# The next image's layer 0 is paced by a line with bends instead of a fixed lead

## The chip, the cores and the metric

The kernel runs on one core of a Trainium2 chip. The metric is the device time of one launch in microseconds. A core has five engines with a queue of their own each: PE (TensorE, matrix products), DVE (VectorE), ACT (ScalarE), POOL (GpSimd) and SP (SyncE, which here only issues DMAs). PEld in the profile is PE's loading of weights, which overlaps its products.

## The reference

The input is four images of 32 by 32 pixels with 384 channels in float32. Four layers follow one another, each of the form `x = x + layer(group_norm(x))`:

```python
x = x + L0(_gn(x))  # deformable attention, 6 heads of 64: q = x@w_q; a grouped 3x3 convolution of q,
                    # LayerNorm, GELU and tanh give an offset per pixel and group; x is sampled
                    # bilinearly there; k, v from the samples;
                    # softmax(q k^T * scale + bias sampled from a table) v; @ w_out
x = x + L1(_gn(x))  # attention, 12 heads of 32, softmax(q k^T) times a weight from sim sim^T, where
                    # sim = sigmoid(cosine of pixels with a strided depthwise convolution), renormalised; @ Wproj
x = x + L2(_gn(x))  # quotient of two box sums (5 pixels along a row, 20 channels)
x = x + L3(_gn(x))  # outlook attention: 9x9 weights per pixel from a softmax, values gathered and
                    # scattered over 3x3 neighbourhoods
```

The layers of one image depend on each other; the images do not.

## The kernel before

All work is written out by Python generators and is unrolled. There are two **lanes**. The front lane (`Front`) computes layer 0. The trunk lane (`Trunk`) computes layers 1 to 3. Image 0 goes through the front lane alone. Then the trunk of image b is issued together with the front of image b+1, for b = 0, 1, 2; the trunk of image 3 runs alone at the end. The front hands its result over in device memory (`x1`): `outputs0` stores it and `Trunk.start` loads it.

A lane is a generator that issues some instructions and then yields a number, its own account of how much it has issued. `Net.layer3` drives both. After each yield of the trunk it adds the number to `done` (as a share of `TRUNK_STEPS` = 1109) and then lets the front issue steps until `ahead` (in shares of `FRONT_STEPS` = 714) has reached a target that depends on `done`. One trunk image is 1.0 of `done`, one front image 1.0 of `ahead`. The order in which instructions are issued here is their priority: a scheduler at compile time keeps to it where it can and lets a later instruction pass one that isn't ready by its own clock. On the chip each engine then works through its list in the fixed order.

The trunk's yields sum up like this (cumulative share of `done` at the end of each stage):

| trunk stage | code | numbers | `done` at its end |
|---|---|---|---|
| norm of x1 | `image` | 15 | 0.0135 |
| inputs of layer 1: Wg product (L400) with depthwise taps on DVE, q, k, v (L1216, L414), norms through device memory | `inputs1` | 158 | 0.156 |
| six pairs of heads, 8 rows of keys each (L1511, L1519, L1541, L1548, L1483), beside the sums for the next pair (L1378, L1386, L1387) | `pair` | 708 | 0.794 |
| output product of layer 1 (L1614) | `out1` | 18 | 0.811 |
| layer 2 (L1656, L1681) | `layer2` | 93 | 0.8945 |
| layer 3: norm, weights and values (L414), sums of weights (L1790), a round trip through device memory (`mt<-skew`), then eight output blocks (L1849) | `layer3` | 15, 30, 20, 20, 8 x 4 | 1.0 |

`Trunk.start(b + 1)` is issued before the eight output blocks.

The front's steps of one image are, in order: `normed` (25: load, transposes L585, group norm), transposes and stores of the sampling source `pairs` (10, L608), q (3 x 5, L400), the grouped convolution (3 x 15, L663), LayerNorm and GELU (25), `positions` (20: about 50 DVE instructions), the first two gathers (8), eight blocks of gather, weighing on DVE and transposes (8 x 7, L735, L748, L762), k and v (30). This is step 234. Then twelve passes of `head0` (one head, half of the queries each): eight blocks (3 each) with a gather by POOL (L827), L840, L844, L845, the product L848 and L849 on DVE; the maximum (3); subtraction L880, exp L881 and products L883 (4 x 2); a store (3). After each second head `over_sums` (2) sends the denominators through device memory and scales (L1128). This is step 696. `outputs0` (3 x 6) applies w_out (L400 `big<-qpad,w`), adds x and stores x1.

Image 1 differs: its `normed` has already been done beside the heads of image 0.

Of the kernel before, what the change touches and what calls it, by code (L numbers as in the profile page):

```python
# [58 lines left out]

TRUNK_STEPS, FRONT_STEPS, LEAD = 1109.0, 714.0, 0.1


def bc(ap, axis, n):
# [7 lines left out]
class Net:  # L73
# [212 lines left out]
    def layer3(self, b, out):  # L286

        for w in self.trunk.image(b, out):
            self.done += w / TRUNK_STEPS
            while self.ahead < self.done + LEAD:  # L290
                self.ahead += next(self.fronts, FRONT_STEPS) / FRONT_STEPS
        assert self.ahead >= min(b + 1, NB - 1)

# [1650 lines left out]
```

## Time and profile before

| | |
|---|---|
| median of 3 runs | 4535.31 us (4531.07 to 4537.83) |
| the profiled execution's own time | 4532.7 us |
| its span, first to last instruction | 4530.9 us |
| busy: PE, DVE, ACT, POOL | 90%, 69%, 51%, 21% |
| mean granted TensorE clock | 0.945 |

The span falls into image 0's front alone (to about 550 us), three stretches of a trunk with the next front (the first Wg product of a trunk stands at 592.5, 1695.3, 2799.9 and 3841.3 us), and the last trunk alone. Every float32 product of 128 x 512 is recorded as two matmul instructions, so a "x24" is twelve products. A matmul's end is modelled and its duration includes the pipeline, so that neighbours in a row overlap; "busy" is the union.

### The profile page before, as it was taken

The numbers are of one execution on the slowest core, as the hardware profiler recorded it, in microseconds if no ns is written. First come the engines' busy times: TensorE is split into PE (matmuls) and PEld (weight loads), VectorE is DVE, ScalarE is ACT, GpSimd is POOL, SyncE is SP. The second block draws the span as 40 slices with busy tenths as digits, with TensorE's granted clock in tenths as the row PEclk, the third lists the DMA queues.
The fourth block names the chain that finished last, engine by engine and source line by source line (L and its number), as shares of the span: only waits on it lengthen the run. The fifth ranks groups of instructions, "written<-read, shape, count | busy, mean of one in ns | idle before, by whom it ended". The sixth has DMA issues, their size and how long they took to land.

```text
span 4530.9 us, 46955 instructions
## 1 busy us (share of the span) xinstructions
PE 4084.6 (90%) x15672; PEld 1735.9 (38%) x15672; DVE 3133.6 (69%) x5925; ACT 2302.5 (51%) x3633; POOL 967.5 (21%) x978
## 2 busy tenths in 40 slices
PE   5599889999999898999999989899999998999998
PEld 2233334333334353433333344343333334344444
DVE  4599555878787727677878753777787874566654
ACT  2176333666665414556666332356566641466632
POOL 1654223212112104211212010422121311000000
PEclk8799899999999998999999989899999998999998
DMA  6445234322212244321322124532122213411011
GB/s 141 145 138 137 80 115 126 86 55 67 67 50 66 73 135 143 110 55 55 85 55 79 39 85 124 164 97 59 43 76 55 78 38 115 121 29 38 22 41 42
DMA packets 235923, 377.28 MB, mean 83 GB/s; under 512 B 117763, under 2 KB 167264, under 8 KB 235680
## 3 DMA queue, kind: packets, MB, share of 16 engines
q1 hardware_dynamic: 183640, 207.55, 16.3%
q0 software_dynamic: 39936, 145.53, 10.9%
q10 hardware_dynamic: 12104, 21.19, 1.4%
q8 instruction: 124, 2.03, 0.2%
q14 instruction: 119, 0.97, 0.1%
HBM read 294.19 MB, written 80.27 MB: 83 GB/s over the span
## 4 chain that ended last, share of the span: by engine, by line
PE 57%; DVE 14%; ACT 6%; issue 6%; DMA 4%; POOL 1%; SPq 0%; another core or an unknown queue 0%; ACTq 0%; DVEq 0%; POOLq 0%
PE bank L1541 13%; PE big L1511 5%; PE big L400 4%; PE bank L414 4%; PE bank L883 4%; PE big L1378 4%; PE bank L848 4%; PE bank L1483 3%; PE bank L1536 3%; PE bank L1216 2%; DVE nmax L1386 2%; ACT big L1387 2%; DVE e L1548 2%; PE big L663 2%; DVE lg L849 1%
## 5 line engine op out<-in xcount | busy, mean ns | idle before, releaser
L1541 PE MATMUL bank<-whole,sg 128*128 128x512 f32 (+3 forms) x2304 | 845.3, 500 | 2.0 <-POOL sg L1494 2.0
L1548 DVE SCALAR_TENSOR_TENSOR e<-bank,gam,e 128x512 f32<-128x512 f32 x768 | 560.5, 747 | 312.5 <-PE bank L1541 176.3
L1387 ACT ACTIVATE big<-big,nmax 128x1024 f32<-128x1024 f32 x384 | 417.5, 1087 | 276.1 <-DVE nmax L1386 264.1
L1519 ACT ACTIVATE e<-big 128x1024 f32<-128x1024 f32 x384 | 380.6, 1019 | 325.5 <-PE big L1511 319.5
L1541 PEld LDWEIGHTS bank<-whole,sg 128*128 128x128 f32 x2304 | 398.2, 195 | 348.1 <-issue 259.7
L1386 DVE TENSOR_REDUCE nmax<-big 128x1 f32<-128x1024 f32 x384 | 452.9, 1218 | 66.8 <-PE big L1378 52.3
L827 POOL DMA_INDIRECT win<-strips,widx x288 | 324.1, 1125 | 706.5 <-DVE z L840 352.2
L1511 PE MATMUL big<-qa,ka 64*128 64x512 f32 x1536 | 432.6, 643 | 22.7 <-ACT big L1387 21.8
L1494 POOL TENSOR_SCALAR sg<-whole,gam 128x512 f32<-128x512 f32 x192 | 143.9, 750 | 1317.3 <-PE bank L1541 1057.7
L1378 PE MATMUL big<-k,q 32*128 32x512 f32 x1536 | 283.4, 654 | 40.9 <-ACT big L1387 21.3
L848 PE MATMUL bank<-qpad,kz 128*128 128x512 f32 x576 | 283.4, 620 | 9.8 <-ACT gn L1553 8.3
L735 POOL DMA_INDIRECT gat<-pairs,sidx x192 | 207.4, 1080 | 385.0 <-DVE ix_gt L516 207.2
L883 PE MATMUL bank<-lg,va 128*64 128x512 f32 x576 | 266.7, 607 | 24.8 <-ACT lg L881 24.8
L883 PE MATMUL bank<-lg,ones 128*64 128x512 f32 x576 | 266.1, 607 | 0.0
L845 DVE SCALAR_TENSOR_TENSOR lg<-z,bias_f,lg 128x512 f32<-128x512 f32 x288 | 218.5, 772 | 58.8 <-ACT lg L844 56.2
L1511 PEld LDWEIGHTS big<-qa,ka 64*128 64x128 f32 x1536 | 138.0, 190 | 278.0 <-issue 123.2
L1483 PE MATMUL bank<-e,vs 128*32 128x512 f32 x1536 | 230.8, 619 | 8.7 <-DVE vs L1477 8.4
L839 ACT ACTIVATE z<-win,bias_f 128x528 f32<-128x528 f32 x288 | 203.6, 735 | 41.6 <-DVE lg L845 21.9
L840 DVE SCALAR_TENSOR_TENSOR z<-win,bias_f,z 128x528 f32<-128x528 f32 x288 | 214.2, 761 | 9.0 <-issue 6.5
L880 DVE TENSOR_TENSOR lg<-lg,tb 128x512 f32<-128x512 f32 x288 | 186.9, 700 | 45.9 <-ACT tb L873 45.9
L849 DVE TENSOR_TENSOR lg<-bank,lg 128x512 f32<-128x512 f32 x288 | 192.1, 684 | 37.6 <-PE bank L848 37.2
L844 ACT ACTIVATE lg<-z,bias_f 128x512 f32<-128x512 f32 x288 | 201.1, 716 | 12.3 <-PE bank L883 5.0
(311 smaller groups left out, 6494.3 us busy)
## 6 DMA issues: line engine op xcount, KB each, us to landing
pairs<-xn SPq DMA_DIRECT2D x64, 192.0 KB
q<-qd SPq DMA_DIRECT2D x48, 256.0 KB
xg<-xgd SPq DMA_DIRECT2D x48, 256.0 KB
w<-in_gmat SPq DMA_DIRECT2D x16, 576.0 KB
w<-in_w_off SPq DMA_DIRECT2D x12, 576.0 KB
w<-in_Wqkv SPq DMA_DIRECT2D x12, 576.0 KB
a<-in_x SPq DMA_DIRECT2D x16, 384.0 KB
x<-a ACTq DMA_DIRECT2D x4, 1536.0 KB
```

Source lines behind the costliest of these rows:

```text
L827: nc.gpsimd.indirect_dma_start(out=win, out_offset=None, in_=self.strips[:, :], in_offset=bass.IndirectOffsetOnAxis(ap=self.widx[:, q, c : ...
L848: nc.tensor.matmul(ps, kz[:, j * P : (j + 1) * P], both, start=True, stop=True)
L849: v.tensor_tensor(lf, ps, lf, ALU.add)
L883: nc.tensor.matmul(po[out, :], w, lf, start=j == 0, stop=j == NJ - 1)
L1378: nc.tensor.matmul(ps[r][:, h * 512 : (h + 1) * 512], self.q4[rows, i * P : (i + 1) * P], self.k4[rows, 0:512], start=True, stop=True,)
L1386: v.tensor_reduce(nmax[:, r, i : i + 1], ps[r], AX.X, ALU.max, negate=True)
L1387: nc.scalar.activation(ps[r], ps[r], AF.Exp, bias=nmax[:, r, i : i + 1], accum_out=den[:, r, i : i + 1],)
L1483: nc.tensor.matmul(av[r0 : r0 + HD1, :], vs[:, r, :], es[h][:, r, :], start=j == 0, stop=j == NJ - 1,)
L1511: nc.tensor.matmul(ps[:, r, :], ka[rows, j * P : (j + 1) * P], qa[rows, cols], start=True, stop=True,)
L1519: nc.scalar.activation(e, ps, AF.Exp)
L1541: last = nc.tensor.matmul(ps[:, (mid - i0) * P :], sg[:, r, m, :], sim[:, h, r, m, (mid - i0) * P :], start=m == 0, stop=m == 1,)
L1548: v.scalar_tensor_tensor(e[:, r, :], ps, self.gam[:, 1:2], e[:, r, :], ALU.add, ALU.mult, accum_out=tot[:, r, h : h + 1],)
```

## The change

Only the target of the front lane changes. Before, it is `done + 0.1` everywhere. After, it is piecewise linear within each image of the trunk. No instruction is added or taken away; their order of issue changes.

```diff
-TRUNK_STEPS, FRONT_STEPS, LEAD = 1109.0, 714.0, 0.1
+TRUNK_STEPS, FRONT_STEPS = 1109.0, 714.0
+PACE = ((0.0, 0.156, 0.795, 0.96, 1.0), (0.03, 0.14, 0.80, 1.0, 1.03))
...
         for w in self.trunk.image(b, out):
             self.done += w / TRUNK_STEPS
-            while self.ahead < self.done + LEAD:
+            share = float(np.interp(self.done - b, *PACE))
+            while self.ahead < b + share:
                 self.ahead += next(self.fronts, FRONT_STEPS) / FRONT_STEPS
```

In front steps (714 to an image; above 714 they belong to the image after the next) the two targets are:

| end of the trunk's stage | `done` | target before | target after |
|---|---|---|---|
| start of the image | 0 | 71 | 21 |
| norm | 0.0135 | 81 | 28 |
| inputs of layer 1 | 0.156 | 183 | 100 |
| pairs | 0.794 | 639 | 571 |
| layer 2 | 0.8945 | 710 | 657 |
| layer 3, weights and values | 0.935 | 739 | 692 |
| layer 3, sums of weights | 0.953 | 752 | 708 |
| layer 3, round trip issued | 0.971 | 765 | 720 |
| end of the image | 1.0 | 785 | 735 |

## The prediction

> **What bounds the kernel now.** I read the page first, then busy time by stage (windows cut at the first Wg product, the first L1541 and the first L1614 of a trunk), then the chain of waits at the ends of the stages, then the waits in the first one.
>
> ```profile
> PE 4084.6 (90%) x15672; PEld 1735.9 (38%) x15672; DVE 3133.6 (69%) x5925; ACT 2302.5 (51%) x3633; POOL 967.5 (21%) x978
> ...
> PE 57%; DVE 14%; ACT 6%; issue 6%; DMA 4%; POOL 1%; SPq 0%; another core or an unknown queue 0%; ACTq 0%; DVEq 0%; POOLq 0%
> ```
>
> PE is first, but holds the chain for only 57% of it. The windows (columns: stretch, length, then busy us of PE, PEld, DVE, ACT, POOL; granted clock; DMA) give the second trunk with a front (rows 1 to 3: inputs of layer 1, pairs, tail), the tail of the third trunk, where no further front follows (row 4), and the last trunk alone (rows 5 to 7):
>
> ```profile
> 1695.30:1828.70 133.40, 114.50 (x328) 48.32 (x324) 98.42 (x172) 57.95 (x96) 60.06 (x61) 0.86 0.50 151
> 1828.70:2558.20 729.50, 683.03 (x2724) 275.04 (x2722) 573.64 (x1126) 449.53 (x716) 152.22 (x153) 0.97 0.24 67
> 2558.20:2799.90 241.70, 212.49 (x831) 106.45 (x827) 116.42 (x195) 66.72 (x94) 22.90 (x15) 0.91 0.32 98
> 3663.50:3841.30 177.80, 157.89 (x516) 79.25 (x513) 105.97 (x176) 53.27 (x70) 14.50 (x9) 0.93 0.25 79
> 3841.30:3939.50 98.20, 95.91 (x281) 39.93 (x281) 47.14 (x73) 41.79 (x66) 9.51 (x16) 0.97 0.44 139
> 3939.50:4382.40 442.90, 438.10 (x2072) 187.83 (x2070) 279.14 (x661) 265.00 (x416) 31.97 (x46) 1.00 0.11 28
> 4382.40:4527.80 145.40, 117.52 (x380) 63.88 (x376) 70.50 (x115) 37.76 (x43) 11.32 (x7) 0.87 0.17 52
> ```
>
> So the front costs 133.4 - 98.2 = 35 us beside the inputs, 729.5 - 442.9 = 287 beside the pairs, 241.7 - 145.4 = 96 in the tail. Alone, inputs and pairs are PE's (98 and 99% busy); the tail leaves PE 28 us and DVE 75 us idle. In the tail with a front, PE has work of the front on the chain:
>
> ```profile
> 1647.29 10.30 PE big L400 x24
> 1657.59 7.89 PE big L663 x72
> 1665.47 9.23 PE bank L1849 x28
> 1674.70 7.89 PE big L663 x72
> 1682.59 3.42 PE bank L1849 x10
> 1686.01 1.46 PE bank L355 x14
> 1687.47 7.89 PE big L663 x72
> ...
> 2158.51 7.02 PE bank L883 x32
> ```
>
> q (L400) and the three convolutions (L663) stand between the trunk's output blocks (L1849) and its Wg, on a full PE: q's 36 records at 10.30/24 = 0.43 are 15.5 us, the convolutions 3 x 7.89 = 23.7, together 39.
>
> Beside the inputs of layer 1 it is different. PE waits there, among others:
>
> ```profile
> POOL gat L735 <- DVE ix_gt L516: 50.4, 1, 50.4
> ...
> PE bank L762 <- DVE xn L751: 10.0, 1, 10.0
> ```
>
> All 48 gathers lie in that window. POOL waits for the positions, DVE for the gathers, and PE's first transpose of the samples for DVE, with the trunk's products behind it in PE's list.
>
> A pass of the heads, by the groups of the page (columns: shapes, count, busy us, mean ns, idle before) and the last line of the chain above:
>
> ```profile
> L845 DVE SCALAR_TENSOR_TENSOR lg<-z,bias_f,lg 128x512 f32<-128x512 f32 x288 | 218.5, 772 | 58.8 <-ACT lg L844 56.2
> L840 DVE SCALAR_TENSOR_TENSOR z<-win,bias_f,z 128x528 f32<-128x528 f32 x288 | 214.2, 761 | 9.0 <-issue 6.5
> L880 DVE TENSOR_TENSOR lg<-lg,tb 128x512 f32<-128x512 f32 x288 | 186.9, 700 | 45.9 <-ACT tb L873 45.9
> L849 DVE TENSOR_TENSOR lg<-bank,lg 128x512 f32<-128x512 f32 x288 | 192.1, 684 | 37.6 <-PE bank L848 37.2
> ```
>
> DVE: 8 x (0.772 + 0.761 + 0.700 + 0.684) = 23.3, with seven maxima of 0.69 and one reduction of 0.7, 29 us. PE: L883 7.0, L848 16 records at 0.43 = 6.9, the maximum's transposes and product 1.3: 15 us. In the trace the pairs run 125 us each with about two passes beside them (77 alone), that is 227 us for ten passes, **22.7 us a pass**. In the tail of row 4, one pass by its DVE work (16 of L880, 10 of L849) and w_out's 36 records (15.5 us) cost 177.8 - 145.4 = 32.4: **17 us a pass**.
>
> A rule bears on this: the Trainium skill, "Perfetto Trace Analysis", section Identifying the Most-Contended Engine, says that the busy share of matmuls is a poor measure of how near PE is to its limit, since matmuls are pipelined. The rows agree: L848 has a mean of 620 ns and a spacing of 0.43 us. Taken at its busy time, PE in the pairs would have 46 us to give and no more.
>
> **The change, part by part.** Instructions and their durations stay. In front steps the targets are 71 before and 21 after at an image's start, 183 and 100 after the inputs, 639 and 571 after the pairs, 785 and 735 at the end. So three packets move, in each of the three stretches:
>
> 1. Steps 21 to 71 (end of `normed`, `pairs`, q, most convolutions) go from the tail to the inputs of the next trunk. Tails 1 and 2 lose 39.6 us of PE on the chain: -79. The first Wg of all (592.5) had q and convolutions ahead of it, 16.6 and 23.3 us of the chain; part of that filled the wait for the norm, so -30.
> 2. Steps 100 to 183 (LayerNorm, `positions`, five of eight gathers; in the trace all gathers) go from the inputs to the pairs. The inputs lose their 35 and gain the 39 of q and convolutions, since PE is full there alone: +4 each, +12. They cost the pairs between 7 (their PE work, two sets of 24 transposes) and 45 (56 us of the front's DVE work in that window at the pairs' 22.7/29). Nearest is the 35 that they cost beside the inputs, with PE's wait of 10 in it; the pairs are longer and the chain has other work beside it, so I take 25.
> 3. 68 steps, that is 68/38.5 = 1.76 passes, go from the pairs to the tail. The pairs give back 1.76 x 22.7 = 40. With the 25 that is -15 each, -45; ends -33 and +5.
>
> The passes' price p in the tail is not in the trace. Half of the 1.76 falls into layer 2 and half into layer 3. From below it is PE's 15, or 10 if layer 3's round trip and norm, where PE waits anyhow, take part of it; from above DVE's 29, or 35 with the waits inside a pass (top, diag, ones, copy: about 4) and a third of `over_sums` (about 6). A gain below zero has no reason, since nothing falls away. I take the 17 of row 4, the same stage: three tails x 1.76 x 17 = +90.
>
> Sum: -30 + 12 - 45 - 79 + 90 = **-52**; as a formula -142 + 5.28 p, zero at p = 27. The profiled execution was 4532.7, so 4481; the median of the runs is 2.6 above it: **4483**.
>
> What is queued where: SP takes the chain of `over_sums` and the x1 stores and reloads amid layer 3's `skew` and `mt` transfers; they used to come during layer 2. Trunk norm, then Wg, wait for x1, now stored just before `start` loads it. In the first stretch that chain, from the store at 539.0 to the end of the group matmuls at 552.6, is 14 us. I cost it at nothing: the output blocks of layer 3 (14 to 15 us of L1849) and its transposes lie beside it. Without that cover it is 14 to 18 in each of three tails. POOL's `sg` for the trunk's rows stands behind 48 gathers of 1.08 us in the pairs now; POOL is 21% busy there, so nothing, unless a gather waits for positions as above.
>
> One rule speaks against the change: the Trainium skill, "TensorE: Matmul & The Clock Gate" (table at its head), has the queues of VectorE, ScalarE and GpSimd as strictly first in, first out. A head's instruction that waits then holds layer 2's behind it. The wait of PE on L762 shows the effect of a fixed order; that DVE has it in layer 2 no row shows. By the rule p would be near 35 and the sum +43.
>
> **The rivals.**
> *DVE sets the tail (slower).* Layer 2 runs serially through DVE, ACT and PE, and a pass is first of all DVE work. In row 4 DVE is busy 106 of 178; with 1.76 passes more, 51 us, and nothing else, it would be 157 of some 208. If each pass goes in series, p = 35: -142 + 185 = +43, **4578**. It decides above p = 27. For it: in row 4's chain, DVE's L849 and L854 alternate with layer 2's. Against it: row 4 measured 17.
> *The lanes pack better.* Pairs hold input work spread over them in place of lumps, and give 30 each; layer 3 hides part of the passes, p = 15: -30 + 12 - 90 - 79 + 79 = -108, **4427**. For it: pair 0 takes 136 us now, the longest, with front steps in lumps of 20 to 30. Against it: the pairs' PE is 94% busy.
> *Nothing happens.* The scheduler lets ready work pass, so the actual order follows readiness rather than the targets: **4535**. Against it: q and convolutions stand in the trace where the target puts them. For it: all gathers ran ahead of theirs.
>
> **How the numbers follow.** The forecast (4440 to 4526) has 0.40, better packing 0.18, no difference 0.09, DVE in the tail 0.33, in which I count the x1 handoff and POOL's order too. A measurement here tells about 0.2%, or 9 us: faster 0.58, same 0.09, slower 0.33. The lower end takes p = 15, the pairs' -33 (-117) and a little more, the upper end p = 35: 4405 to 4578.
>
> **What would show it.** Right: the first Wg at about 562; stretch of the inputs 134 to 140 with PE over 95% busy and no gathers in it; pairs near 715; tails of the first two trunks near 232, of the third near 208. Wrong: DVE above 85% in the tail with longer L1656 to L1681 stretches; `whole<-x` or a PE wait on L355 on the chain ahead of Wg; POOL `sg` late for L1541 in pairs 0 and 1.

## The result and the profile after

The changed kernel takes 4717.27 us (median of 4 runs, 4714.41 to 4719.14) against 4536.06 for the kernel before on the same chip: a ratio of 1.0397, with a 95% interval of 1.0383 to 1.0411. It is slower by 181 us; 52 us faster had been forecast. The profiled span grew by 186 us, from 4530.9 to 4717.2. The changed file is two lines longer ahead of every line named here, so L400 is now L402 and L1849 is L1851.

Page of the kernel after: busy time by engine, then the chain that ended last, by engine.

```profile
PE 4130.1 (88%) x15672; PEld 1738.8 (37%) x15672; DVE 3126.9 (66%) x5925; ACT 2312.9 (49%) x3633; POOL 972.0 (21%) x978
...
PE 51%; DVE 15%; issue 8%; ACT 8%; DMA 4%; POOL 2%; another core or an unknown queue 1%; SPq 0%; DVEq 0%; ACTq 0%; POOLq 0%
```

The instruction counts are the same to the last one, and the busy times nearly so. What changed is the chain: PE has gone from 57% to 51% of it. No engine got more instructions; PE waits more.

Windows of the kernel after, cut at the same places as before (second trunk with a front; tail of the third; last trunk alone):

```profile
1721.50:1872.10 150.60, 141.33 (x563) 58.09 (x563) 65.52 (x107) 61.39 (x101) 9.07 (x16) 0.97 0.46 131
1872.10:2614.90 742.80, 660.85 (x2595) 263.67 (x2594) 540.24 (x1078) 410.01 (x654) 176.66 (x175) 0.95 0.22 62
2614.90:2886.50 271.60, 219.00 (x716) 107.15 (x715) 179.70 (x308) 105.86 (x153) 51.33 (x38) 0.86 0.31 98
3778.80:4026.90 248.10, 206.43 (x659) 96.39 (x658) 172.55 (x290) 101.08 (x142) 46.48 (x35) 0.88 0.30 92
4026.90:4125.60 98.70, 96.41 (x282) 40.00 (x282) 47.10 (x73) 42.10 (x66) 9.49 (x16) 0.97 0.44 142
4125.60:4568.60 443.00, 438.47 (x2070) 187.75 (x2069) 279.15 (x660) 264.39 (x415) 31.82 (x46) 1.00 0.11 27
4568.60:4714.10 145.50, 117.79 (x380) 63.68 (x376) 70.65 (x117) 37.74 (x43) 11.38 (x7) 0.87 0.17 52
```

The last trunk alone is unchanged. In the second stretch the inputs went from 133.4 to 150.6 us, the pairs from 729.5 to 742.8, the tail from 241.7 to 271.6. In the pairs PE has 22 us less to do and the stage is 13 us longer all the same. In this tail the granted clock is lower too, 0.86 against 0.91. That is not the main reason for its growth: of two runs below (e1 and e2), both with 0.90 in this tail, one takes 66 us longer than the other. Over the whole run (first Wg at 552.5):

| | first Wg | inputs 1, 2, 3 | pairs 1, 2, 3 | tails 1, 2, 3 | last trunk |
|---|---|---|---|---|---|
| before | 592.5 | 134.9, 133.4, 135.1 | 730.8, 729.5, 728.6 | 237.1, 241.7, 177.8 | 686.5 |
| after | 552.5 | 150.4, 150.7, 150.1 | 744.6, 742.8, 742.3 | 274.0, 271.6, 248.1 | 687.2 |
| sum of differences | -40 | +48 | +41 | +137 | +1 |

The chain of waits of the kernel after, ahead of the second trunk's Wg (start, length, what):

```profile
1641.89 4.44 PE bank L1792 x36
...
1649.06 4.63 DMA skew<-urow
1653.71 4.41 DMA lg<-rden
...
1658.89 10.17 PE big L402 x16
...
1670.80 4.21 DMA res<-x
...
1676.51 4.03 DMA x<-res
...
1681.11 5.92 DMA a<-in_x
1687.04 0.04 issue
1687.08 4.11 PE bank L587 x18
...
1697.14 3.12 PE bank L357 x14
1700.25 17.18 PE bank L1851 x44
```

Before, q and the convolutions stood between the output blocks there. They are gone: the 44 output blocks run as one piece of 17 us. In their place there is now what the front must do to hand x1 over: denominators (`lg<-rden`), w_out (L402 here), the store and reload of x1, then the next image's load and norm, one after another, 47 us from the first of these to the output blocks.

Chain of the kernel after in the next tail, during layer 2:

```profile
2670.06 1.20 DVE lg L851 x2
2671.26 0.60 DVE rmax L856
2671.86 1.20 DVE t L1651
2673.06 0.60 DVE rmax L856
2673.66 1.20 DVE t L1670
2674.86 0.60 DVE lg L851
2675.47 1.13 DVE d L1671
```

The front's L851 and L856 and layer 2's L1651, L1670, L1671 take turns on DVE, and all of them are on the chain. The window from the output product to Wa, the first product of layer 3, shows how full DVE is there; before first, then after:

```profile
2558.20:2693.00 134.80, 112.79 (x326) 50.80 (x323) 89.93 (x130) 47.88 (x62) 20.27 (x12) 0.92 0.23 78
```

```profile
2614.90:2770.00 155.10, 123.56 (x356) 51.24 (x356) 130.34 (x204) 83.92 (x113) 45.40 (x34) 0.89 0.24 76
```

DVE is busy for 130.3 of 155.1 us, 84%; it was 67%.

The gathers (POOL's timeline of the kernel after: start, us, instruction, idle before it) are now in the first pair, where POOL also makes the trunk's `sg` rows:

```profile
1890.98 1.12 POOL L737 DMA_INDIRECT gat<-pairs,sidx  x1 [9.09 <-DVE ix_gt L518]
...
1912.42 0.95 POOL L737 DMA_INDIRECT gat<-pairs,sidx  x1 [0.30 <-issue]
1913.40 0.70 POOL L1496 TENSOR_SCALAR sg<-whole,gam 128x512 f32<-128x512 f32 x1
1926.31 0.69 POOL L1496 TENSOR_SCALAR sg<-whole,gam 128x512 f32<-128x512 f32 x1 [12.20 <-PE bank L1543]
```

Eighteen gathers run without a break, 1.25 us from start to start, and one `sg` stands behind them. The chain of the same kernel at that place:

```profile
1903.14 1.21 ACT big L1389 x2
1904.35 12.18 another core or an unknown queue
1916.55 1.03 ACT e L1521
1917.62 3.00 PE big L1380 x5
```

There is one core here, so "another core" is a wait whose releaser the records do not give. It ends 2.5 us after that `sg`, and no product of PE is recorded between the two. So that the `sg` is what was waited for is read from the order of the instructions; run e4 below tests it. PE waited 10.9 us ahead of 1917.62. A second run of eighteen gathers from 1972.33 holds two more `sg` until 1997.55, and PE waits 4.6 us.

### The profile page after: what moved, and what is told of

Same layout as the page of the kernel before. It is cut to its first block, busy times and chain, and to the rows that moved or that the text cites. A ratio compares the mean times of both kernels' runs of the same rounds, so it can differ in the third digit from the quotient of the medians.

```text
span 4717.2 us, 46931 instructions
## 1 busy us (share of the span) xinstructions
PE 4130.1 (88%) x15672; PEld 1738.8 (37%) x15672; DVE 3126.9 (66%) x5925; ACT 2312.9 (49%) x3633; POOL 972.0 (21%) x978
## 4 chain that ended last, share of the span: by engine, by line
PE 51%; DVE 15%; issue 8%; ACT 8%; DMA 4%; POOL 2%; another core or an unknown queue 1%; SPq 0%; DVEq 0%; ACTq 0%; POOLq 0%
PE bank L1543 11%; PE big L1513 6%; PE big L402 4%; PE bank L885 4%; PE big L1380 3%; PE bank L850 3%; PE bank L416 3%; DVE nmax L1388 3%; PE bank L1538 3%; PE bank L1485 2%; ACT big L1389 2%; PE bank L1218 2%; DVE e L1550 2%; DVE z L842 2%; PE big L665 2%
## 5 line engine op out<-in xcount | busy, mean ns | idle before, releaser
L1543 PE MATMUL bank<-whole,sg 128*128 128x512 f32 (+3 forms) x2304 | 850.3, 502 | 14.0 <-issue 12.3
L1388 DVE TENSOR_REDUCE nmax<-big 128x1 f32<-128x1024 f32 x384 | 453.4, 1219 | 186.8 <-PE big L1380 177.3
L1543 PEld LDWEIGHTS bank<-whole,sg 128*128 128x128 f32 x2304 | 399.0, 196 | 371.4 <-issue 281.2
L1496 POOL TENSOR_SCALAR sg<-whole,gam 128x512 f32<-128x512 f32 x192 | 133.5, 696 | 1801.2 <-PE bank L1543 1079.5
L829 POOL DMA_INDIRECT win<-strips,widx x288 | 344.0, 1194 | 772.9 <-DVE z L842 423.7
L1513 PE MATMUL big<-qa,ka 64*128 64x512 f32 x1536 | 446.5, 665 | 48.0 <-ACT big L1389 46.3
L1380 PE MATMUL big<-k,q 32*128 32x512 f32 x1536 | 297.7, 660 | 69.4 <-ACT e L1521 39.0
L885 PE MATMUL bank<-lg,va 128*64 128x512 f32 x576 | 289.8, 649 | 38.9 <-ACT lg L883 38.8
L850 PE MATMUL bank<-qpad,kz 128*128 128x512 f32 x576 | 298.8, 644 | 18.3 <-ACT gn L1555 18.3
L885 PE MATMUL bank<-lg,ones 128*64 128x512 f32 x576 | 289.1, 649 | 0.0
L1555 ACT COPY gn<-bank 128x128 f32<-128x128 f32 (+2 forms) x288 | 106.4, 369 | 248.5 <-DVE e L1550 248.0
```

Of the source, the lines that this page charges most:

```text
L829: nc.gpsimd.indirect_dma_start(out=win, out_offset=None, in_=self.strips[:, :], in_offset=bass.IndirectOffsetOnAxis(ap=self.widx[:, q, c : ...
L850: nc.tensor.matmul(ps, kz[:, j * P : (j + 1) * P], both, start=True, stop=True)
L885: nc.tensor.matmul(po[out, :], w, lf, start=j == 0, stop=j == NJ - 1)
L1380: nc.tensor.matmul(ps[r][:, h * 512 : (h + 1) * 512], self.q4[rows, i * P : (i + 1) * P], self.k4[rows, 0:512], start=True, stop=True,)
L1388: v.tensor_reduce(nmax[:, r, i : i + 1], ps[r], AX.X, ALU.max, negate=True)
L1513: nc.tensor.matmul(ps[:, r, :], ka[rows, j * P : (j + 1) * P], qa[rows, cols], start=True, stop=True,)
```

## The experiments

Two theories stood against each other at first. One is the rival of the prediction: each packet of steps carries its own cost, and the head passes in the tail cost far more than 17 us each because DVE sets layer 2. The other is that the handover of x1 and the norm, late now, hold up the next trunk's Wg. Stage times of all runs are in one table behind the experiments; the edits are to the changed kernel unless the text says otherwise. Ratios are against the kernel before on the same chip.

Stage times come from single traces, and the chips differ. The kernel before takes 4536 us on the chip of the result, 4534 to 4535 on those of e5 to e11, but 4510 on the chip of e1 to e4 and 4512 on that of e12; on these two chips there is no trace of it. So a stage of e1 to e4 or e12 set against before or after carries up to some 25 us of a whole run that belong to the chip. Among e1 to e4 this does not arise.

**One packet at a time.** e1 keeps the first packet (q and convolutions beside the inputs), e2 adds the third (heads into the tail), e3 adds the second instead (LayerNorm, positions, gathers into the pairs).

```diff
 e1
-PACE = ((0.0, 0.156, 0.795, 0.96, 1.0), (0.03, 0.14, 0.80, 1.0, 1.03))
+PACE = ((0.0, 0.156, 0.895, 0.93, 1.0), (0.03, 0.256, 0.995, 1.0, 1.03))
 e2
+PACE = ((0.0, 0.156, 0.795, 0.96, 1.0), (0.03, 0.256, 0.80, 1.0, 1.03))
 e3
+PACE = ((0.0, 0.156, 0.25, 0.895, 0.93, 1.0), (0.03, 0.14, 0.35, 0.995, 1.0, 1.03))
```

> The changed kernel with only the first packet moved: each image's front starts at 0.03 and is back on the line before (0.256) when the inputs of layer 1 end, then follows it to the end of layer 2; in layer 3 it stays near 1.0 to 1.03. So q and the convolutions go from the tail to the next inputs; positions, gathers and heads keep their stages. Theory S (the stages add up: the loss of 181 us is packet 2, positions and gathers in the pairs, and packet 3, heads in the tail, about two to one): about 4520 to 4570, near the kernel before, with inputs 20 to 40 longer in each stretch, first Wg at about 553 and tails 40 shorter. Rival H (the handover: what costs is that the front ends just before the next trunk starts and that its normed stands ahead of the output blocks; in this kernel normed still stands there, heads end early): also near 4540. Rival P (q and convolutions beside the inputs are what costs): 4620 and more.

> Packets 1 and 3: as the run with the first packet, but the heads follow the new line from the pairs on (0.80 at 0.795, 1.0 at 0.96); positions and gathers stay beside the inputs of layer 1. Theory S: 4570 to 4620 (60 less in the tail packet than the whole, pairs back below 715 since the inputs' steps are gone from them). Rival H (the tail is everything): 4680 or more. Rival G (POOL's gathers ahead of sg are everything): 4530 to 4550.

> Packets 1 and 2: start at 0.03, 0.14 at the end of the inputs, back on the line before (0.35) at 0.25, that is after seven rows of the first pair, then that line to the end of layer 2, 1.0 to 1.03 in layer 3. So positions and gathers stand in the first pair, but the heads end where they ended before. Theory S: 4630 to 4690, pairs 20 to 40 longer than before in each stretch. Rival H (the tail is everything): 4560 or less. Rival G (gathers ahead of sg): 4680 or more.

Measured: e1 1.0132 (1.0115 to 1.0149), e2 1.0229 (1.0212 to 1.0246), e3 1.0249 (1.0232 to 1.0266). Windows of e1 for the second stretch (inputs, pairs, tail), then the pairs and tail of e2, then the inputs and pairs of e3:

```profile
1672.50:1858.80 186.30, 159.53 (x569) 64.12 (x567) 99.22 (x173) 63.60 (x106) 60.60 (x62) 0.85 0.46 132
1858.80:2589.20 730.40, 682.79 (x2721) 275.04 (x2722) 572.90 (x1124) 448.81 (x715) 152.72 (x153) 0.97 0.23 67
2589.20:2785.80 196.60, 175.83 (x587) 89.55 (x584) 116.20 (x195) 57.79 (x83) 22.31 (x15) 0.90 0.31 99
```

```profile
1870.20:2552.70 682.50, 637.73 (x2586) 258.58 (x2587) 511.67 (x1019) 407.60 (x650) 127.92 (x132) 0.98 0.21 60
2552.70:2815.70 263.00, 214.80 (x721) 102.46 (x720) 175.78 (x299) 102.48 (x150) 50.17 (x37) 0.90 0.33 104
```

```profile
1679.50:1831.40 151.90, 142.83 (x563) 58.94 (x563) 65.59 (x107) 61.52 (x101) 9.07 (x16) 0.96 0.45 131
1831.40:2618.80 787.40, 703.68 (x2740) 283.94 (x2739) 607.58 (x1193) 453.76 (x724) 206.67 (x200) 0.94 0.24 70
```

The first packet, e1 against before: inputs +53 in the second stretch, tail -45. PE's busy time beside the inputs rose by 45 (114.5 to 159.5). Only 35 of that is work of the front: the convolutions (23.9), 24 of q's 36 records (10.5) and three transposes (0.5); q's other 12 records are still in the tail. The remaining 10 are the trunk's own products, the same number of them taking longer: by their lines in the kernel before, L414's 48 records 24.5 us instead of 20.4, L1378's 64 records 18.9 instead of 15.3. Another 8 us is idle time of PE. So a stretch pays more than it gets back, the third tail gives next to nothing back (it never held q or convolutions: 175.3 against 177.8), and the start brings 34. At 4572 the run is 2 us beyond the range of theory S; H and P are further off.

The third packet, e2 against e1: pairs -48, tail +66 in the second stretch (all three: -49, -48, -50 and +70, +66, +65). The pairs give more than forecast; the tail takes a good deal more. Per pass of the target (1.76) that is 38 us in the tail. By DVE work more moved than the target says: in e1, as in the kernel before, the heads had run ahead of the target. The durations of the heads' DVE instructions in the tail sum to 28 us in e1 and 98 in e2, so 70 us or 2.4 passes of 29 moved (DVE's busy time rises by less, 60, since neighbours overlap). By that count a pass costs 28 in the tail and gives 20 in the pairs.

Where in the tail it costs this, the cut at Wa shows (second stretch, us):

| | output product to Wa | DVE busy there | Wa to the next Wg |
|---|---|---|---|
| before | 135 | 67% | 106 |
| e1 | 120 | 70% | 77 |
| e2 | 145 | 88% | 118 |
| after | 155 | 84% | 117 |
| e5 | 221 | 72% | 60 |
| e9 | 149 | 80% | 114 |
| e10 | 134 | 59% | 106 |

From e1 to e2, 25 us come ahead of Wa, where DVE is 88% busy, but 41 come behind it, in layer 3. That is where `over_sums`, w_out and the reload of x1 stand in e2; in e1 w_out comes ahead of Wa.

The second packet, e3 against e1: inputs -34, pairs +57 in the second stretch (all three: -31, -34, -37 and +53, +57, +53). The 35 of the prediction is there; the price is twice the 25 that was taken. All of it stands in the first pair: 195.2 us in e3 against 139.2 in e1, and each of the other five within 1 us of e1's. At 4622 e3 is 8 us below the range of theory S, and outside both rivals'. The three packets by themselves, 1.32% and then 0.97% and 1.17% on top, make 1.0346; the whole change is at 1.0397. The 0.5% between them is what the packets do to one another, or the chip.

**The `sg` rows on DVE.** e4 is the changed kernel with `sg` made by DVE; e7 is the same edit in the kernel before, as a control.

```diff
-            nc.gpsimd.tensor_scalar(
+            v.tensor_scalar(
```

> The changed kernel with the scaling of sg (L1496) on DVE in place of POOL, so that the trunk's products no longer wait behind a run of gathers in POOL's list. The work is the same. If PE's waits in the first pair (about 11 at 1906 and 5 at 1994 us in the profile after, slices with 13 to 14 of 25 us busy) come from sg behind the gathers, the pairs lose 15 to 30 in each stretch and gain some DVE work (48 x 0.4 to 0.7 an image): 4640 to 4690 in all. If they come from the gathers' own latency or from DVE, no gain: 4717 to 4800.

> Control for the run with sg on DVE: the kernel before with the same edit. In it no gather of samples stands among the pairs, only the heads' window gathers. If what the edit gained in the changed kernel (about 46 us) is the samples' gathers ahead of sg, it gains little here: 4490 to 4540 against 4510. If any gather on POOL holds sg back, it gains as much here: 4450 to 4480.

Measured: e4 1.0298 (1.0276 to 1.0319), e7 1.0018 (1.0005 to 1.0031). The edit costs the kernel before 0.2% and gains the changed one 1.0% (1.0397 to 1.0298). It is in the pairs: 718.4, 716.6, 716.6 against 744.6, 742.8, 742.3, and there in the first pair, which holds the gathers: 126.2 us after and 103.1 in e4 (second stretch), the other five pairs together 616.6 and 613.5. So `sg` waiting behind gathers is shown; its size less well. The first pair gives 21 to 23 us a stretch, but the changed kernel was not run on e4's chip, and the ratios leave 45 us for the whole run, 15 a stretch (18, if the 8 us that the edit costs the kernel before are added). On one chip, the second packet costs the pairs 53 to 57 with `sg` on POOL (e3 against e1) and 33 to 37 with `sg` on DVE (e4 against e2). Some 20 us a stretch fits all of these.

**Is it the handover, or the norm?** e5 ends the heads with layer 2, so that `over_sums`, w_out and the stores of x1 come before layer 3 instead of amid it. e6 takes away the lead at an image's start, so that the next image's `normed` has no place ahead of the output blocks by the target.

```diff
 e5
+PACE = ((0.0, 0.156, 0.795, 0.8945, 1.0), (0.03, 0.14, 0.80, 1.0, 1.03))
 e6
+PACE = ((0.0, 0.156, 0.795, 0.96, 1.0), (0.0, 0.14, 0.80, 1.0, 1.0))
```

> The changed kernel with the bend at 0.96 moved to 0.8945: as many heads leave the pairs as in the change, but all of them stand in layer 2, and over_sums, w_out and the x1 stores come before layer 3 instead of amid it. On this chip the changed kernel would be at about 4690 by its ratio. Theory H (the handover: in the tail after, some 50 us between the last head product and the output blocks hold two DMA round trips, the reload of x1, and the next image's normed one behind the other): tails 20 to 35 shorter than the changed kernel's 248 to 273, 4590 to 4630 in all. Rival D (the passes' own work on DVE in layer 2): the same passes on less room, tails as long or longer, 4690 to 4740.

> The changed kernel with no lead at an image's start (0.0 in place of 0.03, 1.0 in place of 1.03): normed of the image after the next is issued after the trunk's norm instead of before the output blocks of layer 3. If its chain (load, transposes, statistics, group product) is what holds the output blocks back, tails 1 and 2 lose 15 to 25 and the third stays; the inputs may gain 5 to 20 since normed and its stores now precede q: 4650 to 4700. If it only fills waits there: tails unchanged, inputs longer, 4700 to 4750.

Measured: e5 1.0421 (1.0403 to 1.0438), e6 1.0365 (1.0343 to 1.0386). In e5 the layer 3 part of the second tail is short again: 60 us from the first Wa to the next Wg, against 117. But from the output product to Wa it now takes 221 us instead of 155, and the whole is longer:

```profile
2605.30:2886.30 281.00, 219.12 (x716) 108.53 (x715) 184.31 (x308) 105.39 (x153) 51.03 (x38) 0.85 0.31 97
```

e6 left the tails at 271.9, 272.0 and 246.3. So the place of the handover is not what makes the tail long, and `normed` ahead of the output blocks is not either. But e5 moved the handover, it did not remove it: in its second tail Wa starts 67 us after layer 2's last product (L1681 in the kernel before, where it is 27 us), at 2826.6. Ahead of it stand the last head products (to 2775), w_out (to 2805) and the next image's transposes (2814 to 2819). DVE is busy for only 72% ahead of Wa there. So the time by which this chain holds up the trunk remains a rival to DVE's work, and no run takes it out.

**How much of the pass's price is DVE's?** e9 and e10 leave out the subtraction of L880 (a fifth of a pass's DVE work) in the changed kernel and in the kernel before; the exponential takes the first query's maximum as a bias for all queries of a pass.

```diff
-            v.tensor_tensor(lf, lf, tb, ALU.subtract)
-            nc.scalar.activation(lf, lf, AF.Exp)
+            nc.scalar.activation(lf, lf, AF.Exp, bias=tb[:, 0:1])
```

> The changed kernel without the heads' subtraction on DVE (L882, 8 x 0.69 us = 5.5 us of a pass's 29) in images 1 to 3: the exponential takes one constant for all queries of a pass (the first query's maximum, as its bias) in place of each query's own maximum, so it still waits for the same tile; softmax is the same up to rounding. Theory D (DVE sets layer 2's part of the tail, at 0.85 us per us of DVE work): with 3.4 passes there the tails lose 13 to 19 each, and of that most between out1 and the product with Wa; the pairs with 8.6 passes lose 25 to 40 by the price of 20.5 us a pass. 4560 to 4620 where the changed kernel is 4715. Rival L (the chain inside a pass, maximum to product, or PE sets it): tails lose under 6, since this chain loses one 0.7 us step; 4640 to 4715.

> The same edit in the kernel before, with one pass in the tail and 10.4 in the pairs. Theory D: tails lose 3 to 6, pairs 30 to 50, all together 110 to 160: ratio 0.965 to 0.976. Then the gap between the two kernels narrows by 20 to 45 us, since fewer DVE steps stand in the tail. Rival L: tails 0 to 6 as well, pairs under 15, gap unchanged: ratio 0.99 or more.

Measured: e9 1.0274 (1.0256 to 1.0292), e10 0.9917 (0.9900 to 0.9934). Second tail of e9, then of e10:

```profile
2578.40:2841.70 263.30, 214.66 (x715) 105.91 (x714) 161.56 (x276) 106.12 (x153) 48.70 (x38) 0.88 0.32 102
```

```profile
2536.00:2776.20 240.20, 210.36 (x831) 106.05 (x827) 106.08 (x178) 67.76 (x94) 22.81 (x15) 0.91 0.32 98
```

In the changed kernel DVE's busy time in a tail fell by 18 us (179.7 to 161.6 in the second) and the tails by 8.1, 8.3 and 12.5: 28.9 of 54, or 0.53 us for a us of DVE's busy time. In the kernel before it fell by 10 in each tail, and the tails moved by +1.2, -1.5 and +0.1: nothing. The pairs gave 36 of 120 in e9 and 30 of 139 in e10: 0.30 and 0.22 (the profiled execution of e10 was 11 us slower than its median). So DVE work in the tail has a price after the change and had none before. But it is about half its length, not all of it: by this price the 25 us of DVE's busy time that a pass brings to the tail (60 for 2.4 passes) account for 13 of its 28. DVE alone does not set the tail. By their times both runs lie in the ranges of rival L; e9's tails lie between the two theories.

**The line the other way.** e8 keeps a straight line with a lead of 0.15. e11 asks for the heads earlier, out of the tail and into the pairs.

```diff
 e8
+PACE = ((0.0, 1.0), (0.15, 1.15))
 e11
+PACE = ((0.0, 0.156, 0.75, 0.9, 1.0), (0.1, 0.256, 0.95, 1.0, 1.1))
```

> The straight line with a lead of 0.15 in place of 0.10: everything in the opposite direction of the change. By the prices measured (a pass costs 37 in the tail and 27 in the pairs; LayerNorm and positions cost 35 beside the inputs and 55 beside the pairs; q and convolutions 43 in the tail and 53 beside the inputs) less stands in the dear places: 4470 to 4505. Rival: the next image's positions and gathers then stand between the round trip of layer 3 and the next Wg and lengthen it: 4520 to 4570.

> The kernel before with the third packet in the opposite direction: 0.10 and 0.256 as before, then 0.95 at 0.75 and 1.0 at 0.9, so heads leave the tail for the pairs. By the prices of the run with packets 1 and 3 (27 us a pass in the tail, 20.5 in the pairs) a pass moved gains 6 and at most about one is left to move: 5 to 20 us less in three stretches, ratio 0.995 to 0.999. If the pairs are full, as PE's 94% says, they lengthen by the pass's 22 to 29 us instead: ratio 1.000 to 1.006.

Measured: e8 0.9985 (0.9973 to 0.9998), e11 1.0165 (1.0144 to 1.0187). e8 moved 36 steps from each place to the one before it: inputs +21 to +35, pairs -9 to -17, tails -9 to -22, nearly nothing in sum, and less than the 0.2% that a measurement can tell. The 4470 to 4505 that the prices had given is missed; 4530 lies in the rival's range. e11 misses both of its ranges. Its pairs and tail in the second stretch:

```profile
1853.00:2627.60 774.60, 714.98 (x2807) 280.91 (x2807) 597.85 (x1165) 461.13 (x738) 154.50 (x155) 0.97 0.23 63
2627.60:2841.90 214.30, 187.21 (x744) 99.53 (x740) 89.49 (x154) 53.52 (x71) 18.84 (x13) 0.89 0.37 111
```

The tails gave 22, 27 and 17, but the pairs took 42, 45 and 46 more, for about 0.9 of a pass by DVE work (the heads' instructions sum to 344 us instead of 318 in the second stretch). A pass taken out of the pairs gave 20; a pass put in cost some 50. Among the paces tried the straight line is the best, and the mean of 22.7 a pass was not the price of one more.

**The second packet by itself, spread out.** e12 keeps the first and third packets where they were, holds back LayerNorm, positions and gathers, catches up over four pairs instead of one, and makes `sg` on DVE as e4 does.

```diff
-PACE = ((0.0, 0.156, 0.795, 0.96, 1.0), (0.03, 0.14, 0.80, 1.0, 1.03))
+PACE = ((0.0, 0.156, 0.6, 1.0), (0.1, 0.14, 0.7, 1.1))
```

> Packet 2 by itself, with both other packets where they were before: the target is 0.1 at a trunk image's start, 0.14 at the end of the inputs of layer 1 (all of LayerNorm, positions and gathers come later), and is back at done + 0.1 only at done = 0.6, so that what is held back spreads over four pairs; and the trunk's sg rows are made by DVE, so that POOL's gathers have nothing of the trunk behind them. Theory that packet 2 loses through the queue on POOL and through its lump in pair 0: without both, the inputs lose 35 us a stretch, as they did between e1 and e3, and the pairs take 25, the price of the prediction: 3 x (-10), and the control's +8 for sg on DVE, is -22 of 4535, ratio 0.993 to 0.998, pairs 750 to 757. Rival, that any uneven load of the pairs costs more than an even one, whatever the queue (in the run with the heads earlier, pairs rose by 44 us for one pass more): pairs +45 or more, ratio 1.008 to 1.018, with DVE over 85% busy in the pairs that hold the most. In both, the tails stay at 237, 242 and 178 and the first Wg at 590.

Measured: 1.0219 (1.0205 to 1.0233); inputs 131.6, 133.4, 133.5, pairs 769.7, 763.2, 763.2, tails 236.8, 236.5, 176.9. Both theories missed the inputs, which gained next to nothing. The chain shows why (start, length, what), and then the window of the same time:

```profile
1820.01 3.37 DVE a L498
1823.40 3.35 DVE ix_th L499
1826.76 1.13 DVE nmax L1388
1827.89 3.26 DVE a L498
1831.24 3.31 DVE ix_th L499
```

```profile
1801.00:1840.00 39.00, 19.90 (x68) 9.54 (x67) 36.23 (x79) 18.90 (x36) 0.54 (x1) 0.65 0.16 50
```

By the target the positions belong to pair 0. The order on the chip has them ahead of the first L1543 all the same (that the scheduler took them because they were ready is likely, not shown), and the trunk's `nmax` (L1388) stands between them in DVE's list: DVE is 93% busy there and PE half idle. The pairs rose by 34 to 39 us and nothing came back. That is past the ratios of both theories and nearer to the rival. Pair by pair (second stretch, e12 against before): 107.3 and 136.2, 155.0 and 127.7, 132.3 and 118.5, 149.5 and 126.7, 124.3 and 125.1, 94.8 and 95.3. The rival's sign, DVE over 85%, is there in the fourth pair (132.4 of 149.5 us, 89%), but not in the second, which rose most (114.7 of 154.9, 74%). Why the spread load costs as much as it does is not settled.

Stage times of the runs (us; the three stretches):

| run | first Wg | inputs | pairs | tails |
|---|---|---|---|---|
| e1 | 558.4 | 186.6, 186.3, 187.1 | 731.3, 730.4, 733.6 | 196.1, 196.6, 175.3 |
| e2 | 553.9 | 183.6, 184.9, 188.4 | 681.9, 682.5, 683.3 | 265.9, 263.0, 240.0 |
| e3 | 550.2 | 155.6, 151.9, 150.3 | 784.6, 787.4, 786.2 | 189.1, 191.3, 178.3 |
| e4 | 550.9 | 152.0, 151.3, 151.3 | 718.4, 716.6, 716.6 | 275.5, 265.5, 248.7 |
| e5 | 549.2 | 151.0, 150.1, 150.4 | 737.9, 736.7, 739.3 | 280.4, 281.0, 245.9 |
| e6 | 550.0 | 150.8, 149.2, 149.2 | 739.1, 739.2, 739.1 | 271.9, 272.0, 246.3 |
| e7 | 589.1 | 136.2, 131.7, 136.6 | 731.1, 731.4, 737.3 | 240.1, 241.3, 177.8 |
| e8 | 593.7 | 169.7, 156.2, 155.8 | 713.8, 713.2, 719.9 | 221.6, 220.0, 169.3 |
| e9 | 549.7 | 151.9, 151.4, 153.5 | 730.2, 729.4, 733.7 | 265.9, 263.3, 235.6 |
| e10 | 589.1 | 138.0, 133.7, 138.2 | 715.7, 721.1, 721.6 | 238.3, 240.2, 177.9 |
| e11 | 588.9 | 138.1, 137.8, 137.9 | 772.6, 774.7, 774.4 | 215.4, 214.3, 161.0 |
| e12 | 581.2 | 131.6, 133.4, 133.5 | 769.7, 763.2, 763.2 | 236.8, 236.5, 176.9 |

No pace was faster than the line before by more than a measurement can tell. The fastest kernel here, e10, owes that to the subtraction left out, not to the order.

## Why the prediction was wrong, step by step

By the stages, forecast and measured differ by 126 us in the tails (+11 forecast, +137 measured), 86 in the pairs (-45, +41), 36 in the inputs (+12, +48) and -10 at the start. So two terms failed above all: the price p of a head pass in the tail, and the price of the second packet in the pairs.

- **The start**, -30: it was -40. The 39.9 of q and convolutions were on the chain in full, and nothing filled the wait for the norm.
- **The inputs**, +4 each: +15 to +17. The loss of 35 was right in size (e3 against e1: -34). The gain of 39 was 53 (e1), though only 35 us of the front's PE work had come: 10 went into the trunk's own products taking longer, 8 into waits. That PE's added work adds its own length and no more was the error.
- **The pairs**, -15 each: +13 to +14. The gain of 40 was there and more (48 to 50, e2 against e1). **The price of the second packet failed**: 25 was taken, e3 shows 53 to 57, beyond the upper bound of 45. Some 20 of it is the queue on POOL (e4); the rest stays open. The prediction named that queue and costed it at nothing because POOL is 21% busy, "unless a gather waits". Gathers did wait, but what cost was their coming in runs: eighteen at 1.25 us hold one small `sg` for up to 22 us, and a mean of 21% says nothing about that. The Trainium skill, "TensorE: Matmul & The Clock Gate" (table at its head), which the prediction used against DVE alone, gives GpSimd's queue as strictly first in, first out too, and POOL's timeline above agrees.
- **The tails**, -79 for q and convolutions: e1 shows -41 and -45, or -86. The size was right; the chip's 25 us a run and q's 12 records that stayed leave the reason less sure.
- **A pass in the tail**, p = 17: **this was the largest miss**. e2 against e1 gives 38 for each of the 1.76 passes, above the end of 35, and 28 by the 2.4 that moved. The row that the value was taken from, tail 3 of the kernel before, is a stage where DVE's work has room: e10 takes 10 us out of it and the tail does not move. With 60 us of busy time more, e9 shows 0.53 us for each. The marginal price was read from a stage with slack, and applied to one without.
- **The number of passes**, 1.76, came from the targets. The trace of before had the heads ahead of them, so 2.4 moved. The prediction had noted the same of the gathers and not followed it for the heads.
- **The handover of x1**, costed at nothing: it stands on the chain, 47 us of it, as the sign "a PE wait on L355 ahead of Wg" would have it. Of the 66 us that the third packet adds to a tail, 41 come behind Wa, where it stands. e5 moved it ahead of Wa and the tail stayed as long. So its place is not the cause; whether its length is part of the other half of p stays open.
- **The rival "DVE sets the tail"** had the sign and part of the place, at 4578. With 38 for 35, the inputs' +48 for +12 and the pairs' +41 for -45 its sum goes past 4700. Its reason was half right: DVE is 84% busy from the output product to Wa, close to the sign of 85%, and a us of its busy time cost about half a us in the tail. The Trainium skill, "Perfetto Trace Analysis", section Identifying the Most-Contended Engine, calls VectorE's occupancy a fair measure of how near it is to its limit; here, at 84%, half of a pass's price went with DVE's work. The other half was not taken apart. A fixed order of short steps that wait for one another across engines would do it, as the alternating lines of the chain suggest, and so would the chain of the handover; no run took either away alone.
- **"Better packing"** did not occur: pairs 3 to 5 of the second stretch took 131.6, 129.0 and 132.1 us against 118.5, 126.7 and 125.1 before. The front's PE work in them rose from 33.0, 33.1 and 33.4 to 39.6, 36.2 and 38.7, since the first two pairs held gathers and positions in place of heads.

## What to carry to other kernels

When work moves between stages, its price must be read at the margin of the stage it goes to, with the amount that goes there: the same head pass cost 17 us in a tail with slack and 28 in a tail with two passes more; it gave 20 when taken out of the pairs and cost some 50 when put into them. An engine that is idle on average still blocks, if what is put on it comes in runs: look at the longest run that can stand ahead of a short instruction with someone waiting. And count what moves from the trace's order, not from the program's targets, wherever a scheduler stands between them.

## What the runs showed of the hardware that was not expected

Indirect gathers leave POOL at 1.25 us from start to start (0.95 busy and 0.30 of issue), so eighteen of them close POOL's queue for 22 us. And idle time of PE was not to be had by giving it more products: in e1's inputs PE got 35 us of the front's work in a stage with 19 us of its time idle (133.4 long, 114.5 busy), and ended with 27 idle (186.3 and 159.5), its other products 10 us slower. The granted clock was 0.86 and 0.85 in these two, and 0.97 in the inputs of the changed kernel, which wait for no gathers.
